# Context products of the first attention in two runs, and its running maxima read from the score banks

## The chip, the cores and the metric

The kernel runs on one core of a Trainium2 chip. The core has five engines that run beside each other and meet only at semaphores: TensorE (in the profile PE, with its weight loads apart as PEld), VectorE (DVE), ScalarE (ACT), GpSimd (POOL) and SyncE (SP), which here only starts transfers. [...] The metric is the time of one execution on the device, in microseconds.

## What is computed

The whole model has six layers. An input x of 16 samples with 64 rows of 512 passes through a cross-attention over a context (16 samples, 1601 keys of 256), a state-space layer, a routed feed-forward layer, a second cross-attention, a causal self-attention and a quantised gated feed-forward layer; each adds its result to x. The change touches only the first:

```python
def _L0_xattn_ref(q, k, v, Wq, bq, Wk, bk, Wv, bv, Wo, bo):
    HEADS, D_MODEL = 16, 512
    D_K = D_MODEL // HEADS
    B, LQ, _ = q.shape
    LKV = k.shape[1]
    qh = (q @ Wq + bq).reshape(B, LQ, HEADS, D_K).transpose(0, 2, 1, 3)
    kh = (k @ Wk + bk).reshape(B, LKV, HEADS, D_K).transpose(0, 2, 1, 3)
    vh = (v @ Wv + bv).reshape(B, LKV, HEADS, D_K).transpose(0, 2, 1, 3)
    scores = jnp.einsum('bhqd,bhkd->bhqk', qh, kh) * (1.0 / np.sqrt(D_K))
    attn = jax.nn.softmax(scores, axis=-1)
    out = jnp.einsum('bhqk,bhkd->bhqd', attn, vh)
    return out.transpose(0, 2, 1, 3).reshape(B, LQ, D_MODEL) @ Wo + bo
...
x = x + _L0_xattn_ref(_layernorm(x, axis=-1), ctx_512, ctx_512, ...)
```

## The kernel before, in words

All arithmetic is in fp32. The first attention is worked off in 32 units. Unit `u` is sample `u // 2` and one half of its heads, eight heads with 64 queries each, so a row of 512 scores per key. The 1601 keys are cut into 13 chunks `k` of 128 (the last has 65); keys lie on the partitions, and the tile `st` holds all scores of a unit as 13 chunks of 512 columns. There are two such tiles, so two units are in work at once.

The loop over `u` (its body begins at `for u in range(U + 1)`) is a pipeline over neighbouring units. In one turn the kernel builds the keys, values and scores of unit `u`, and finishes the softmax and the context of unit `u - 1`. The order of the instructions on each engine is written out by hand: `pin` keeps what it wraps in the order of the program. Every engine works strictly in that order, so an instruction that waits holds up all that is behind it on its engine.

One turn, in program order:

- `k_proj(u, i, z)` (L204 on TensorE, L218 on ScalarE): eight key products of 400 columns, each emptied by ScalarE into `kt`. Among them: `maxima(u-1)` transposes the running maxima on TensorE (L295) and VectorE reduces them over the keys (L297); `shift(u-1)` spreads the negated maxima on TensorE (L304) and VectorE adds them to the scores (L310); `exps(u-1, k)` takes the exponentials of two chunks on ScalarE (L318), and GpSimd adds them up in `acc` (L323, L325, L327). `divide(u-2)` (L351, L352) writes the normalised context of the unit before.
- `v_proj(u, k)` (L204, L229): 13 value products of 256 columns, each emptied by VectorE into `vt`. Key and value products share the two PSUM banks of the pool `ps_mm`, so a product starts only when the one before the last has been emptied.
- `scores(u, g)` (L204 on TensorE, tile `sc`): three groups of four chunks. A group fills four banks; then ScalarE copies it into `st` in two halves `r`, of four heads each (L264). The third group also does the short chunk 12 in `scl` (L268).
- `running_max(u, k)` on VectorE: the maximum over chunks, kept in `rm` as two chunks wide. `k == 2` starts it from chunks 0 to 3 (L284); 4, 6, 8 and 10 take two more chunks each from `st` (L286); 12 takes the short one (L289); L500 folds the two halves.
- `attend(u-1, i)` (tile `av<-st,vt`): context products, 13 chunks x 4 heads for each of the two halves `i`, each half 104 matmuls in the profile. Tiles of 32 columns of the array make them short. `sum_up(u-1)` adds the row sums from `acc` (`av<-acc,ones`), after L488 has folded `acc`.
- Beside that, one piece of the last layer's weights is quantised per turn: `piece_load` (SyncE), `piece_scale` (L164, L165, L166 on VectorE, L167 on GpSimd), `piece_round` (L171), `piece_store` (L175 on GpSimd, then SyncE).
- In seven of the turns `project(g)` takes two finished samples through the output projection (`ps<-wo,xnT`, L360) with the statistics of the next normalisation.

Every f32 matmul of keys, values, scores and context appears as two rows of the profile, so "x32" is a group of 16. [...]

## Time and profile before

| what | time |
|---|---|
| three timed runs, median (lowest to highest) | 2096.86 us (2092.23 to 2099.53) |
| the profiled execution itself | 2094.09 us |
| its span, first to last instruction | 2092.4 us |
| mean granted TensorE clock over the span | 0.985 |
| one ordinary unit, from first scores to first scores | 34.98 us |
| in that unit, busy: TensorE / VectorE / ScalarE / GpSimd | 33.41 / 27.60 / 17.05 / 19.73 us |
| mean of one maximum from `st` (L286, 128 of them) | 1678 ns |
| mean of one addition on GpSimd (L325, 124 of them) | 2575 ns |
| mean of one copy of scores (L264, 192 of them) | 1016 ns |

Rows of the profile give the line, the engine, the operation, output and inputs by tile name, the shape, the count, then busy time and the mean of one, and the idle time of the engine just before them with what ended it. A releaser "issue" means that the profile shows nothing that the engine waited for. In a timeline each row has start, duration, engine, line, operation, count, and in brackets the idle time before it. The loop over units runs from about 59 to 1215 us.

### The profile page before, as it was taken

What the parts mean: (1) busy time and instruction counts of PE and PEld (TensorE: products, weight loads), DVE (VectorE), ACT (ScalarE), POOL (GpSimd) and SP (SyncE); (2) the same over time, 40 slices, a digit from 0 to 9 for tenths busy, and PEclk for the clock granted to TensorE, in tenths of its full rate; (3) what the DMA queues carried; (4) which work ended last, traced back from release to release, by engine and by line L of the source; (5) the groups of instructions that cost most, each with busy time, mean ns of one, the idle gap of its engine ahead of it and who ended that gap; (6) DMA issues with size and microseconds to landing.
All of it is one profiled execution on the core that took longest, in us unless ns stands there. A gap on an engine that the chain in (4) does not pass through costs nothing. (4 is left out here: it accounts for less than half of the span.)

```text
span 2092.4 us, 39026 instructions
## 1 busy us (share of the span) xinstructions
PE 1958.8 (94%) x17197; PEld 1237.7 (59%) x17197; DVE 1262.7 (60%) x1741; ACT 801.3 (38%) x1112; POOL 713.1 (34%) x463
## 2 busy tenths in 40 slices
PE   8899999999999999999999799899999999999779
PEld 4677777677767677776767654444454455444334
DVE  2587778787787877787777844721113234428751
ACT  2445354545445453544445443210101133316700
POOL 0356555464546565564656421200003000000100
PEclk9999999999999999999999999999999999999879
DMA  5011001101110110111010120420227971200001
GB/s 204 21 54 43 32 32 53 43 17 48 43 53 11 53 43 22 43 50 46 12 53 11 37 102 22 168 76 19 94 67 280 347 295 61 71 0 11 20 0 40
DMA packets 61754, 141.13 MB, mean 67 GB/s; under 512 B 4448, under 2 KB 31600, under 8 KB 60432
## 3 DMA queue, kind: packets, MB, share of 16 engines
q1 hardware_dynamic: 61584, 138.63, 18.5%
q8 instruction: 135, 2.21, 0.4%
q14 instruction: 35, 0.29, 0.0%
HBM read 127.02 MB, written 11.60 MB: 66 GB/s over the span
## 5 line engine op out<-in xcount | busy, mean ns | idle before, releaser
L204 PE MATMUL ps<-wkv,ctxT 128*128 128x256 f32 (+1 forms) x1664 | 399.9, 388 | 26.9 <-DVE vt L229 25.6
L204 PE MATMUL ps<-ctxT,wkv 128*128 128x400 f32 (+1 forms) x1024 | 365.6, 504 | 9.7 <-DMA ctxT<-in_ctxT_dram 7.6
L204 PEld LDWEIGHTS ps<-wkv,ctxT 128*128 128x128 f32 (+1 forms) x1664 | 295.9, 185 | 107.4 <-DVE vt L229 38.0
L325 POOL TENSOR_TENSOR acc<-acc,st 128x1024 f32<-128x1024 f32 x124 | 319.3, 2575 | 23.6 <-ACT st L318 18.6
L218 ACT ACTIVATE kt<-ps,cols 128x400 f32<-128x400 f32 (+1 forms) x256 | 152.1, 594 | 372.5 <-PE ps L204 372.5
L229 DVE TENSOR_TENSOR vt<-ps,rows 128x256 f32<-128x256 f32 (+1 forms) x416 | 170.4, 420 | 183.9 <-PE ps L204 183.7
L264 ACT COPY st<-sc 128x1024 f32<-128x1024 f32 x192 | 185.0, 1016 | 246.8 <-PE sc L204 246.8
L204 PEld LDWEIGHTS ps<-ctxT,wkv 128*128 128x128 f32 x1024 | 190.0, 191 | 138.1 <-issue 9.3
L310 DVE TENSOR_TENSOR st<-st,nb 128x1024 f32<-128x1024 f32 (+1 forms) x224 | 239.1, 1139 | 34.6 <-PE nb L304 34.6
L318 ACT ACTIVATE st<-st 128x1024 f32<-128x1024 f32 (+1 forms) x224 | 215.9, 994 | 10.7 <-DVE st L310 10.4
L286 DVE TENSOR_TENSOR rm<-rm,st 128x1024 f32<-128x1024 f32 x128 | 214.8, 1678 | 2.2
L204 PEld LDWEIGHTS sc<-qd,kt 64*128 64x128 f32 x3072 | 178.9, 188 | 36.8 <-issue 24.5
L204 PE MATMUL sc<-qd,kt 64*128 64x128 f32 x3072 | 197.3, 278 | 2.1 <-ACT st L264 2.1
L323 POOL TENSOR_TENSOR acc<-st 128x1024 f32<-128x1024 f32 x31 | 73.4, 2367 | 311.0 <-issue 192.7
L204 PE MATMUL av<-st,vt 128*32 128x64 f32 x6656 | 106.8, 221 | 27.0 <-issue 18.0
L204 PEld LDWEIGHTS av<-st,vt 128*32 128x32 f32 x6656 | 98.5, 111 | 35.7 <-issue 26.7
L59 PE MATMUL ps<-xnT,w 128*128 128x512 f32 x256 | 112.2, 594 | 0.0
L59 PE MATMUL ps<-w,hT 128*128 128x512 f32 x256 | 110.2, 592 | 0.0
L167 POOL TENSOR_TENSOR w<-w,winv 128x512 f32<-128x512 f32 x36 | 48.4, 1346 | 163.6 <-DVE winv L166 152.8
L1200 POOL TENSOR_TENSOR gate<-up,gate 128x1024 f32<-128x1024 f32 x4 | 9.5, 2387 | 260.0 <-ACT up L1199 260.0
L276 POOL COPY qd<-xnT 32x128 f32<-32x128 f32 x128 | 79.4, 621 | 37.4 <-DVE xnT L395 32.4
L59 PE MATMUL po<-wdT,gate 128*128 128x512 f32 x192 | 85.4, 608 | 3.2 <-DVE gate L1222 3.2
(236 smaller groups left out, 2306.4 us busy)
## 6 DMA issues: line engine op xcount, KB each, us to landing
cT<-in_ctxT_dram SPq DMA_DIRECT2D x16, 1601.0 KB, 9.6
cN<-in_ctx_dram SPq DMA_DIRECT2D x16, 1536.0 KB, 9.8
ctxT<-in_ctxT_dram SPq DMA_DIRECT2D x15, 1601.0 KB, 7.3
grid<-w SPq DMA_DIRECT2D x36, 256.0 KB, 2.0
w<-grid SPq DMA_DIRECT2D x36, 256.0 KB, 2.7
w<-in_w_dram SPq DMA_DIRECT2D x2, 4096.0 KB
mk<-kept SPq DMA_DIRECT2D x16, 512.0 KB, 3.6
w<-in_wgate_dram SPq DMA_DIRECT2D x12, 256.0 KB, 3.2
```

The lines of the kernel that those rows point to most:

```text
L59: pe.matmul(out, lhsT=lhsT, rhs=rhs, start=start, stop=stop)
L167: pin(gp.tensor_tensor(w, w, inv.unsqueeze(2).to_broadcast([P, 16, 32]), ALU.mult))
L204: pin(pe.matmul(out, lhsT=lhsT, rhs=rhs, start=start, stop=stop))
L218: pin(s.activation(kts[u, i][:, o:o + n], ps[:, :n], AF.Identity, bias=col(C_BK0 + c)))
L229: pin(v.tensor_tensor(t[:n, :], ps[:n, :], row(R_BV0 + e, 256)[:n, :], ALU.add))
L264: pin(s.copy(st[:, ks[0]:ks[-1] + 1, r * 256:(r + 1) * 256], sc[:, r]))
L276: pin(gp.tensor_copy(qds[u % 2][r, :, (j % 2) * LQ:(j % 2 + 1) * LQ], qo[r, c:c + 2, b * LQ:(b + 1) * LQ]))
L286: pin(v.tensor_tensor(rms[u], rms[u], f[:, k:k + 2, :], ALU.max))
L310: pin(v.tensor_tensor(f[:m, k:k + n, :], f[:m, k:k + n, :], nb[:m].unsqueeze(1).to_broadcast([m, n, 512]), ALU.add))
L318: pin(s.activation(f[:m, k:k + n, :], f[:m, k:k + n, :], AF.Exp))
L323: pin(gp.tensor_tensor(accs[u], f[:, 0:2, :], f[:, 2:4, :], ALU.add))
L325: pin(gp.tensor_tensor(accs[u], accs[u], f[:, k:k + 2, :], ALU.add))
```

## The change

The score tile of a group becomes two tiles of two banks, one for each half `r`. The first group is treated as before. In the second and third group, VectorE no longer takes the maxima of chunks 4 to 11 from `st` but from the score banks, four instructions of 128x512 per group. Two engines don't read one tile at once: ScalarE copies half 1 while VectorE reads half 0, then they change over. The context products of half `i = 0` move from behind the third group to behind the second. The last exponentials of `u - 1` (chunk 12) move ahead of the second group's copies, and the fold of `acc` ahead of `piece_scale`.

```diff
-            sc = ps_sc.tile([P, 2, 4, 2 * P], F32, name="sc", tag="sc")
+            sc = [ps_sc.tile([P, 4, 2 * P], F32, name="sc", tag=f"sc{r}") for r in range(2)]
...
             for k in ks:
-                one_chunk([sc[:, r, k - ks[0], :] for r in range(2)], k)
+                one_chunk([sc[r][:, k - ks[0], :] for r in range(2)], k)
             if last == ks[-1] + 1:
                 tail = [ps_mx.tile([P, 2 * P], F32, name="scl", tag="mx"),
                         ps_mm.tile([P, 2 * P], F32, name="scl", tag="mm")]
                 one_chunk(tail, last)
-            for r in range(2):
-                pin(s.copy(st[:, ks[0]:ks[-1] + 1, r * 256:(r + 1) * 256], sc[:, r]))
+
+            def keep(r):
+                pin(s.copy(st[:, ks[0]:ks[-1] + 1, r * 256:(r + 1) * 256], sc[r]))
+
+            if g == 0:
+                keep(0)
+                keep(1)
+                return
+
+            keep(1)
             if last == ks[-1] + 1:
                 n = nkeys(last)
                 for r in range(2):
                     pin(s.copy(st[:n, last, r * 256:(r + 1) * 256], tail[r][:n]))
+            for r in range(2):
+                rm = rms[u][:, :, r * 256:(r + 1) * 256]
+                for z in (0, 2):
+                    pin(v.tensor_tensor(rm, rm, sc[r][:, z:z + 2, :], ALU.max))
+                if r == 0:
+                    keep(0)
...
                 pin(v.tensor_tensor(rms[u], f[:, 0:2, :], f[:, 2:4, :], ALU.max))
-            elif k + 1 < KC:
-                pin(v.tensor_tensor(rms[u], rms[u], f[:, k:k + 2, :], ALU.max))
             else:
...
             next_v(0, 1)
             scores(u, 0)
-            next_exps(2)
+            next_exps(3)
             next_v(2, 3, 4, 5)
             running_max(u, 2)
...
             scores(u, 1)
-            next_exps(1)
+            if old:
+                attend(u - 1, 0)
             next_v(6, 7, 8, 9)
-            running_max(u, 4)
-            running_max(u, 6)
-            if u < NPREP:
-                piece_scale(u, pin)
             if old:
                 acc = accs[u - 1]
                 pin(v.tensor_tensor(acc[:, 0], acc[:, 0], acc[:, 1], ALU.add))
+            if u < NPREP:
+                piece_scale(u, pin)
             if old and u <= NPREP:
                 piece_store(u - 1, pin)
             scores(u, 2)
             if old:
-                attend(u - 1, 0)
                 attend(u - 1, 1)
                 sum_up(u - 1, [(accs[u - 1][:, 0], P)])
-            running_max(u, 8)
-            running_max(u, 10)
             next_v(10, 11)
             running_max(u, 12)
```

## The prediction

> **What bounds the kernel now.** I read the shares of busy time first: TensorE is busy for 94% of the span (page line below), and the stretch from 100 to 1200 us, which is the first attention's loop, has 1051.6 us of matmul time in 1100.0 at a granted clock of 1.00. So the loop runs at the pace of TensorE, and a gain can only come from its idle time there. The list of waits in that stretch says whom it waits for (engine and line, released by whom: total us, times, longest):

> ```profile
> PE 1958.8 (94%) x17197; PEld 1237.7 (59%) x17197; DVE 1262.7 (60%) x1741; ACT 801.3 (38%) x1112; POOL 713.1 (34%) x463
> ...
> PE ps L204 <- DVE vt L229: 23.7, 24, 1.6
> ...
> PE av L204 <- issue: 18.9, 18, 1.7
> ```

> Two causes make almost all of it: value products that wait for VectorE to empty their bank, and a gap inside the context products. The timeline of one unit (start, duration) shows how they hang together:

> ```profile
> 557.85 2.06 PE L204 MATMUL sc<-qd,kt 64*128 64x128 f32 x32
> ...
> 563.03 5.67 POOL L325 TENSOR_TENSOR acc<-acc,st 128x1024 f32<-128x1024 f32 x2 [0.42 <-ACT st L318]
> ...
> 563.48 2.06 PE L204 MATMUL sc<-qd,kt 64*128 64x128 f32 x32
> ...
> 563.93 2.53 DVE L284 TENSOR_TENSOR rm<-st 128x1024 f32<-128x1024 f32 x1
> ...
> 565.47 3.72 PE L204 MATMUL ps<-wkv,ctxT 128*128 128x256 f32 x16
> ...
> 569.12 2.06 PE L204 MATMUL sc<-qd,kt 64*128 64x128 f32 x32
> ...
> 571.54 3.12 PE L204 MATMUL av<-st,vt 128*32 128x64 f32 x208
> ...
> 573.93 4.05 DVE L286 TENSOR_TENSOR rm<-rm,st 128x1024 f32<-128x1024 f32 x2
> ...
> 574.81 1.99 PE L204 MATMUL ps<-wkv,ctxT 128*128 128x256 f32 x8
> ...
> 577.91 0.74 DVE L229 TENSOR_TENSOR vt<-ps,rows 128x256 f32<-128x256 f32 x2
> 578.37 1.08 PE L204 MATMUL ps<-wkv,ctxT 128*65 128x256 f32 x4 [1.57 <-DVE vt L229]
> ```

> Call the start of the first scores (557.85) zero. The second scores start at 5.63, the third at 11.27, the context products at 13.69, value products 10 and 11 at 16.96. At 8 x 0.216 us of pitch, product 12 could start at 18.69. It starts at 20.52, because VectorE is in the last two maxima (4.05 us) and empties product 10 only at 577.91. The loss is **1.83 us per unit**. Another unit shows the gap:

> ```profile
> 645.24 0.59 PE L204 MATMUL av<-st,vt 128*32 128x64 f32 x26 [0.97 <-issue]
> ...
> 648.31 1.08 PE L204 MATMUL ps<-wkv,ctxT 128*65 128x256 f32 x4 [0.28 <-DVE vt L229]
> ```

> Its scores began at 627.81, so product 12 is at 20.50 again: the gap only eats up the wait. Taking the gap alone away would bring nothing; VectorE ends this stretch either way.

> **The change, part by part.** TensorE, GpSimd and SyncE keep their instructions (GpSimd's and SyncE's orders are untouched); of the 208 context products, 104 move behind the second scores. Per unit VectorE trades four 128x1024 maxima from SBUF for eight 128x512 ones that read PSUM.

> *Price of a maximum.* The old ones take 1687 ns on average, but the very first unit, with GpSimd idle, has the like at 1.23:

> ```profile
> 63.28 1.23 DVE L284 TENSOR_TENSOR rm<-st 128x1024 f32<-128x1024 f32 x1 [3.58 <-ACT st L264]
> ```

> The nearest row of the new form is L360, x<-x,ps 128x512, SBUF and PSUM operands: 686 to 689 ns in all 8, also where GpSimd adds beside it. A dependent VectorE instruction follows 0.035 behind, an independent one overlaps by 0.08 (rows L164, L165; L229). From the first of a group's four to the next eviction: 0.725 + 0.61 + 0.725 + 0.61 = **2.67 us**. Bounds: 2.3 (no better than four halves of the 1.13 pitch of L310) and 3.3 (half of 1687 each). I take 2.67. [...] New maxima have one SBUF input, and evictions of that kind keep 0.42 us in the middle of GpSimd's adds.

> *Second group.* Context half: 104 x 14.1 ns (2.93 us for 208) = 1.47. Scores at 5.63, context from 7.61, value products 6, 7 and 8 due at 9.13, 10.04 and 10.95. VectorE is still in L284 until 8.61, then runs the four maxima from 8.65, and empties product 6 at 11.32 to 11.74; product 8, in the same bank, starts at 11.78. Before, this eviction came at once. So **0.83 us of new stall** stands at product 8; third scores at 13.60 instead of 12.77.

> *Third group.* Tail scores 15.49, second context half 16.02, sums 17.49, product 10 at 17.82, product 12 due at 19.55. VectorE: evictions 8 and 9 until 14.2, the add of acc and the weight piece's scaling (0.63 + 1.15) until 15.85, maxima until 18.5, so it waits for product 10 and no stall is left. Product 12 starts at 19.55, 0.97 earlier. What is late next: the tail maximum and L500's fold (0.78 + 0.69) after eviction 11 end at 21.72; the transposes are due at 21.82 (k product after 0.92, 1.35 long). Before, they began at 22.79. I keep **0.9 us** per ordinary unit. From there the rest hangs on TensorE and just moves.

> *Units with an output projection* (7 of them): in the one begun at 662.77, second scores start at 9.07 and transposes at 26.84. By the same steps, the third scores come at 16.21, product 12 at 22.17, transposes at 24.44. The projection's VectorE work ends when the second scores do (about 11.2), so maxima end early enough that product 8 loses at most 0.1. Gain about **2.2 us** each.

> *New waits.* The third maximum waits for ScalarE's copy of its bank (ends 8.75 and 16.6; VectorE gets there at 9.98 and 17.2). ScalarE's held-back copy waits for the second maximum (10.0 and 17.2) and ends at 11.0 and 18.3. Behind it stand the next group's copy (15.6) and the k evictions (about 22); third scores need it at 13.6. All have over a microsecond, except that third maximum in group three, 0.6.

> *Moves at nothing.* The last exponential goes before the second copies: ScalarE is idle from 5.99 to 7.74 and it takes 0.64; the context half needs it at 7.61. Without that cover: 0.6 per unit. The add of acc moves ahead of the scaling; GpSimd's adds end at about 12.2, VectorE is there at 14.1. If GpSimd were late, scaling, maxima and evictions 10 and 11 would queue behind it. The scaled piece reaches GpSimd about 0.2 later, and its store and the next load on SyncE as much, with most of a unit to spare.

> *The gap.* A unit has 412 matmuls and as many loads, 824 instructions; the 135 packets of 16.4 KB on the instruction queue make about 255 TensorE instructions each. 824 is three packets and 56 more, and the gap indeed moves by about 30 products from unit to unit (after 202, 172, ...). It comes only when a packet's worth lies in the dense products (1.8 us). Halved, a packet spans at least 2.8 us; durations plus gaps ask for 2.2 to 3.2. I cost it at nothing. [...]

> **Sum.** 24 ordinary units x 0.9 = 21.6, 7 x 2.2 = 15.4, the first unit (no context products) about nothing: 37 us. The profiled execution took 2094.09 (span 2092.4), 2.8 under the median of 2096.86. 2094.1 - 37 = 2057; I say **2058**, between that and 2060 from the median.

> **Rivals.**
> - *Dearer maxima*: 3.3 us per group puts 0.6 more on product 8 in 24 units and some in the others, 18 in all: about 2076. For it: no row has exactly this form. Against: L360.
> - *The gaps stay*: another 18 or so lost, 2076. For it: half a run is still dense. Against: 2.8 us per packet.
> - *No stall at product 8*: if L284 gets ahead of GpSimd (1.23 instead of 2.53), 20 more are won: 2038. Against: GpSimd's pair starts at 5.18, L284 at 6.08, unit after unit.
> [...]
> - *The change isn't there*: the instruction orders show both halves and all eight maxima.

> **How the numbers follow.** Forecast 0.55 (own range 2049 to 2067), dearer maxima 0.12, gaps 0.08, no stall 0.07, lock or another wait that I don't see 0.18. The range 2038 to 2082 leaves that last one out. A measurement of this kernel tells about 0.3% (6 us) from no change; 0.04 of the favourable cases falls there: faster 0.78, same 0.04, slower 0.18.

> **What would show it.** Right: maxima of 0.69 us, product 8 waiting 0.7 to 0.9 for VectorE, no wait at product 12, no gaps among the context products, transposes about 0.9 earlier after a unit's first scores. Wrong: maxima over 0.85 us, gaps of a microsecond, or ScalarE's held-back copy delaying third scores.

## The result and the profile after

The change makes the kernel faster: the median of six runs is **2062.36 us** (2059.99 to 2070.21), against 2097.11 (2092.23 to 2099.53) in six runs of the kernel before. The ratio is 0.9842, with a 95% interval of 0.9823 to 0.9861. The medians are 34.7 us apart. The profiled execution took 2065.08 us (span 2063.4), which is 29.0 less than the profiled execution before; the sum of the prediction, 37, was made against that one. The profiled execution before was 3.0 faster than its median, the one after 2.7 slower, and the account below is of these two.

Of the 29.0, the loop holds 27.9. From the first unit's transposes of the maxima to the last unit's, 1115.7 us went by before, 1089.0 now, and the first transposes start 1.2 earlier. Over the same stretch (to the start of the last unit's first transpose) these are the length, then the busy time of TensorE, its weight loads, VectorE, ScalarE and GpSimd, and the granted clock, before and after:

```profile
80.55:1195.78 1115.23, 1068.87 (x12853) 793.76 (x12851) 868.89 (x1110) 539.49 (x727) 632.54 (x386) 1.00 0.10 36
...
79.34:1167.91 1088.57, 1068.47 (x12853) 792.15 (x12851) 824.00 (x1234) 542.69 (x727) 544.90 (x386) 1.00 0.11 37
```

TensorE is as busy as before, to 0.4 us; its idle time fell from 46.4 to 20.1, and these 26.3 are nearly all of the 26.7 by which the stretch is shorter. A unit's length, taken from its transposes to those of the next:

| interval between transposes (us) | before | after |
|---|---|---|
| ordinary units (22) | 34.98, four of them 35.93 to 36.04 | 34.22 to 34.30, the same four 34.98 to 35.29 |
| five of the seven with a projection | 38.08 or 38.09, one 39.04 | 36.77 to 36.83, one 37.72 |
| the other two with a projection | 39.04, 39.04 | 36.77, 36.77 |
| the unit behind each of these two | 35.93, 36.41 | 36.37, 36.83 |

The page of the kernel after, first busy times, then the row of the new maxima:

```profile
PE 1957.7 (95%) x17197; PEld 1236.0 (60%) x17197; DVE 1216.9 (59%) x1869; ACT 804.8 (39%) x1112; POOL 622.3 (30%) x463
...
L280 DVE TENSOR_TENSOR rm<-rm,sc 128x512 f32<-128x512 f32 x256 | 168.5, 679 | 10.7 <-PE sc L204 3.8
```

The line numbers have moved: L280 are the new maxima from the banks, L299 is the first group's maximum (L284 before), L331 the exponentials (L318), L338 GpSimd's additions (L325), L308 the transposes (L295), L509 the fold (L500); in the experiments some shift by a few lines. VectorE has 128 instructions more and 45.8 us less busy time: eight maxima of 679 ns replace four of about 1680. GpSimd's instructions are the same ones, and took 713.1 us before; what goes with that is seen in the part on the rivals. The list of waits in the kernel after, loop only (engine and line, released by whom: total us, times, longest):

```profile
PE ps L204 <- DVE vt L229: 14.9, 24, 0.6
...
PEld mt L308 <- DVE rm L509: 9.6, 30, 0.5
...
PEld av L204 <- issue: 5.3, 31, 0.2
```

Value products used to wait 23.7 us for VectorE; it is 14.9 now, one wait of 0.6 in each of 24 units. The gaps among the context products, 18.9 us before, are gone: only 0.2 at the first weight load of a run is left. The timeline of one ordinary unit of the kernel after (start, duration) shows where the wait has gone:

```profile
545.51 2.06 PE L204 MATMUL sc<-qd,kt 64*128 64x128 f32 x32
...
550.67 5.66 POOL L338 TENSOR_TENSOR acc<-acc,st 128x1024 f32<-128x1024 f32 x2 [0.40 <-ACT st L331]
...
551.14 2.06 PE L204 MATMUL sc<-qd,kt 64*128 64x128 f32 x32
...
551.59 2.52 DVE L299 TENSOR_TENSOR rm<-st 128x1024 f32<-128x1024 f32 x1
...
553.13 1.66 PE L204 MATMUL av<-st,vt 128*32 128x64 f32 x104
...
554.22 2.73 DVE L280 TENSOR_TENSOR rm<-rm,sc 128x512 f32<-128x512 f32 x4
...
556.86 0.75 DVE L229 TENSOR_TENSOR vt<-ps,rows 128x256 f32<-128x256 f32 x2
...
557.34 1.99 PE L204 MATMUL ps<-wkv,ctxT 128*128 128x256 f32 x8 [0.62 <-DVE vt L229]
...
559.26 2.06 PE L204 MATMUL sc<-qd,kt 64*128 64x128 f32 x32
...
563.49 2.86 PE L204 MATMUL ps<-wkv,ctxT 128*128 128x256 f32 x12
...
567.53 0.60 PE L308 MATMUL mt<-ident,rm 128*128 128x128 f32 x4
```

Read it from the wait in the middle. Product 8 (557.34) waits for an eviction, that is, for VectorE to empty product 6's bank (556.86). VectorE could not do that one sooner because it was in the four maxima of group two (554.22), and these began late because L299 had VectorE until 554.11. L299 runs beside GpSimd's pair of additions (550.67), as it did before. Product 10 to product 12, the place of the old stall, is now one unbroken run of 12 rows (563.49). So the stall was cut and moved from the third group to the second.

### The profile page after: what moved, and what is told of

It reads as the page before. It is cut to its first block, busy times and chain, and to the rows that moved or that the text cites. A ratio compares the mean times of both kernels' runs of the same rounds, so it can differ in the third digit from the quotient of the medians.

```text
span 2063.4 us, 39030 instructions
## 1 busy us (share of the span) xinstructions
PE 1957.7 (95%) x17197; PEld 1236.0 (60%) x17197; DVE 1216.9 (59%) x1869; ACT 804.8 (39%) x1112; POOL 622.3 (30%) x463
## 3 DMA queue, kind: packets, MB, share of 16 engines
q1 hardware_dynamic: 61584, 138.63, 18.9%
q8 instruction: 135, 2.21, 0.5%
## 5 line engine op out<-in xcount | busy, mean ns | idle before, releaser
L204 PE MATMUL ps<-wkv,ctxT 128*128 128x256 f32 (+1 forms) x1664 | 399.7, 388 | 16.5 <-DVE vt L229 16.3
L204 PE MATMUL ps<-ctxT,wkv 128*128 128x400 f32 (+1 forms) x1024 | 365.6, 503 | 12.7 <-DMA ctxT<-in_ctxT_dram 8.8
L204 PEld LDWEIGHTS ps<-wkv,ctxT 128*128 128x128 f32 (+1 forms) x1664 | 295.9, 185 | 96.2 <-DVE vt L229 26.8
L338 POOL TENSOR_TENSOR acc<-acc,st 128x1024 f32<-128x1024 f32 x124 | 319.6, 2577 | 23.0 <-ACT st L331 17.9
L265 ACT COPY st<-sc 128x1024 f32<-128x1024 f32 x192 | 191.7, 1016 | 320.5 <-PE sc L204 284.3
L229 DVE TENSOR_TENSOR vt<-ps,rows 128x256 f32<-128x256 f32 (+1 forms) x416 | 170.7, 421 | 202.0 <-PE ps L204 201.8
L204 PEld LDWEIGHTS ps<-ctxT,wkv 128*128 128x128 f32 x1024 | 189.7, 191 | 141.3 <-issue 12.8
L331 ACT ACTIVATE st<-st 128x1024 f32<-128x1024 f32 (+1 forms) x224 | 212.1, 992 | 7.3 <-DVE st L323 6.9
L204 PEld LDWEIGHTS sc<-qd,kt 64*128 64x128 f32 x3072 | 179.2, 188 | 36.5 <-issue 24.2
L204 PE MATMUL sc<-qd,kt 64*128 64x128 f32 x3072 | 197.8, 278 | 1.6 <-ACT st L265 1.6
L280 DVE TENSOR_TENSOR rm<-rm,sc 128x512 f32<-128x512 f32 x256 | 168.5, 679 | 10.7 <-PE sc L204 3.8
L204 PE MATMUL av<-st,vt 128*32 128x64 f32 x6656 | 108.7, 223 | 8.8 <-DVE xnT L365 8.8
L204 PEld LDWEIGHTS av<-st,vt 128*32 128x32 f32 x6656 | 98.5, 112 | 18.1 <-ACT st L331 9.1
L167 POOL TENSOR_TENSOR w<-w,winv 128x512 f32<-128x512 f32 x36 | 37.9, 1055 | 192.3 <-DVE winv L166 181.7
L59 PEld LDWEIGHTS ps<-w,hT 128*128 128x128 f32 x256 | 48.6, 190 | 61.2 <-issue 61.2
```

What stands on the lines that cost most here:

```text
L59: pe.matmul(out, lhsT=lhsT, rhs=rhs, start=start, stop=stop)
L167: pin(gp.tensor_tensor(w, w, inv.unsqueeze(2).to_broadcast([P, 16, 32]), ALU.mult))
L204: pin(pe.matmul(out, lhsT=lhsT, rhs=rhs, start=start, stop=stop))
L229: pin(v.tensor_tensor(t[:n, :], ps[:n, :], row(R_BV0 + e, 256)[:n, :], ALU.add))
L265: pin(s.copy(st[:, ks[0]:ks[-1] + 1, r * 256:(r + 1) * 256], sc[r]))
L280: pin(v.tensor_tensor(rm, rm, sc[r][:, z:z + 2, :], ALU.max))
```

## Experiments

Each kernel was timed beside runs of the kernel before. For the first four that ran (the context split alone, the maxima alone, both halves behind the second scores, values first) that took 2096.86 us, for the others 2094.97. Beside the medians I use the loop's length in the profile, first transposes to last: 1115.7 us before, 1089.0 after.

### One half of the change alone

*The context split without the new maxima.* The kernel before, with one half of the context behind the second scores and the exponentials moved ahead:

```diff
-            next_exps(2)
+            next_exps(3)
...
             scores(u, 1)
-            next_exps(1)
+            if old:
+                attend(u - 1, 0)
...
             if old:
-                attend(u - 1, 0)
                 attend(u - 1, 1)
```

> The kernel before, with only the context half i = 0 moved behind the second scores (and the last exponentials ahead of it); the maxima still come from st. Theory (VectorE's turn ends the stretch): the third scores start 1.5 us later, VectorE's chain behind them (two pairs of maxima of about 2.5 and 4.05 us, the scaling, the fold) begins later by as much, and product 12 starts at about 22.0 after the first scores of a unit instead of 20.52. 24 units x 1.5 and 7 x 0.5: about 2136 us, with no gaps left among the context products. Rival (the gain comes from breaking up the dense run): the gaps go and up to 19 us are won, 2078 to 2090.

It took 2168.17 us, ratio 1.0335 (1.0293 to 1.0378). The timeline of one of its units:

```profile
593.22 2.06 PE L204 MATMUL sc<-qd,kt 64*128 64x128 f32 x32
...
610.56 4.05 DVE L286 TENSOR_TENSOR rm<-rm,st 128x1024 f32<-128x1024 f32 x2
...
614.53 0.74 DVE L229 TENSOR_TENSOR vt<-ps,rows 128x256 f32<-128x256 f32 x2
615.00 1.08 PE L204 MATMUL ps<-wkv,ctxT 128*65 128x256 f32 x4 [1.95 <-DVE vt L229]
```

Product 12 starts 21.78 us after the unit's first scores, where the theory had 22.0 and the kernel before 20.52. The reason is seen in the rows: the pair of maxima (4.05 us) still stands ahead of the eviction, and TensorE has less context left with which to cover it. The unit is 36.24 long where nothing else disturbs it, 1.26 more than before; 31 such units are the 39 us of the theory. (This edit leaves the fold of `acc` behind the weight piece's scaling, so the sums also wait 0.53 for it in each unit; VectorE's eviction ends later still.) The measured loop is 77.2 longer, and the remaining 38 were on the list of neither theory. The granted clock in this loop is 0.97 and not 1.00, and 3.2% of its 1192 us is 38. The experiment on the clock comes back to it.

*The new maxima without the split.* The kernel after, with both halves of the context behind the third scores:

```diff
             scores(u, 1)
-            if old:
-                attend(u - 1, 0)
             next_v(6, 7, 8, 9)
...
             if old:
+                attend(u - 1, 0)
                 attend(u - 1, 1)
```

> The kernel after, with the context half i = 0 moved back behind the third scores. Theory: without 1.5 us of context products between the second scores and product 6, product 8 is due at 9.4 and still waits for VectorE until 11.8, a stall of 2.4 us; the whole run of context products is dense again, VectorE no longer hides its gaps, so about 1 us comes on top in some 18 units. Product 12 at about 21.1 in units without a gap against 20.52 before: 24 x 0.55 + 18 - 3 makes about 2125 us. Rival (cheaper maxima alone pay): VectorE's relief of 1.8 us per unit shows as time, 2060 to 2080.

It took 2157.65 us, ratio 1.0291 (1.0265 to 1.0317). In the timeline of a unit, the wait at product 8:

```profile
596.15 2.88 PE L204 MATMUL ps<-wkv,ctxT 128*128 128x256 f32 x8 [2.22 <-DVE vt L229]
```

The four maxima are the same as in the kernel after, but no context product lies between scores and value products, so TensorE stands for 2.2 us instead of 0.6. The dense run of 208 context products is back too, and with it 18.9 us of gaps in the list of waits. Each half alone is about 3% slower than the kernel before, and a good part of that is a lowered clock (below: 1.95% is left of the maxima's 2.9% when it is kept up); together they are 1.6% faster. The maxima free VectorE at the end of the unit and load it in the middle; the context half fills the middle.

### Where the context products stand, and the gaps

*Both halves behind the second scores*, which makes the run of 208 whole again but leaves everything else as it is after the change:

```diff
             if old:
                 attend(u - 1, 0)
+                attend(u - 1, 1)
             next_v(6, 7, 8, 9)
...
             if old:
-                attend(u - 1, 1)
                 sum_up(u - 1, [(accs[u - 1][:, 0], P)])
```

> The kernel after, with both context halves behind the second scores, so 208 in one run. Theory on the gaps (an instruction packet that lies in the dense run takes longer to come than to be used): gaps of about a microsecond return among the context products in some 18 of 31 units, VectorE's chain behind is moved by each, and about 15 to 19 us are lost against the kernel after: 2078 to 2082. Product 8 no longer waits, but product 12 does, by about as much, so units without a gap keep their length. Rival (the gaps came from something at the end of the unit, not from density): no gaps, 2055 to 2063.

It took 2091.76 us, ratio 0.9975 (0.9965 to 0.9985); almost all of the gain is gone. Its list of waits in the loop:

```profile
PE av L204 <- issue: 18.9, 21, 1.4
```

and the timeline of a unit with such a gap:

```profile
563.51 2.66 PE L204 MATMUL av<-st,vt 128*32 128x64 f32 x174
...
567.32 0.72 PE L204 MATMUL av<-st,vt 128*32 128x64 f32 x34 [1.15 <-issue]
```

The gap is inside the run, no data is waited for, and it stands in 21 units of 31. Ordinary units without one are 33.98 long in most cases, 0.24 shorter than in the kernel after; those with a gap of 0.3 to 0.6 us are 34.6 to 34.8, those with one of 0.8 to 1.2 are 35.2 to 35.6. The same products in two runs have none, and no version with two runs showed one. So in these kernels the length of the dense run decides on the gap.

What goes with a gap is seen in the transfers of the trace. The page has a DMA queue of kind "instruction" with 135 packets, 2.21 MB, so 16.4 KB each. In each of the 18 gaps of the kernel before and the 21 of this one, exactly one such packet lands 1.2 to 1.6 us before the gap ends; the same holds for the 20 and 18 gaps of the two kernels of the next section. A moment taken at random stands at that distance from a packet in 4% of cases. From the start of the packet to the end of the gap 2.2 to 2.9 us go by. That agrees with gaps that are waits for instructions, as the prediction worked out from its counts; no run changed the packets themselves, so it is not shown as the cause.

The loss is 29 and not the 15 to 19 that I had expected: a unit with a gap is longer by more than the gap lasts. I put that down to the place of the gap, ahead of evictions, so that VectorE's work is pushed back with it; that is not shown.

### What lowers the clock

In the loop of maxima_only TensorE is busy for 1097.6 us with the work for which the kernel before takes 1068.9, and the granted clock is 0.98. About a microsecond after the end of the wait above the clock falls to half, for 3.41 us; that is why the eight rows took 2.88 us and not 1.99. Of 24 waits of 2.2 us in the loop, 16 are followed by such a drop; of seven with 1.2 to 1.3, none. These 16 drops cost about 27 us (16 x 3.41 at half speed).

Why 16 of 24? The drops lie on a fixed grid: in all ten traces every change of the granted clock stands within 0.004 us of a multiple of 3.413 us, counted from the first. Here is the step of the grid that holds the wait above and the step behind it, then two such steps around another wait (columns: stretch, its length, busy time of TensorE, its weight loads, VectorE, ScalarE and GpSimd with counts, granted clock, DMA share, GB/s):

```profile
593.69:597.10 3.41, 1.19 (x6) 0.87 (x5) 2.67 (x6) 1.01 (x1) 2.72 (x2) 1.00 0.00 0
597.10:600.51 3.41, 3.41 (x19) 2.54 (x19) 1.86 (x4) 0.00 (x0) 0.00 (x0) 0.50 0.02 5
214.84:218.25 3.41, 1.44 (x7) 0.94 (x5) 3.24 (x6) 1.61 (x2) 3.33 (x2) 1.00 0.00 0
218.25:221.66 3.41, 3.17 (x30) 2.68 (x32) 2.08 (x6) 0.00 (x0) 0.58 (x1) 1.00 0.00 0
```

Both waits last 2.2 us, but the second one lies across the edge of two steps: its part in this one is 1.94 us. Counted by steps, the loops of all ten traces agree. Each of the 38 drops (16 here, 22 in split_only, behind waits of 1.95 us) follows a step in which TensorE stood idle for 1.95 us or more, and no step with 1.94 or less has a drop behind it.

To see whether it is the standing still that does it, I took maxima_only and put four more matmuls between value products 7 and 8. They write to the context bank, which the context products then overwrite, and so add work and no result:

```diff
-            next_v(6, 7, 8, 9)
+            next_v(6, 7)
+            if old:
+                avs[u - 1] = ps_av.tile([P, 2, 2, LQ], F32, name="av", tag="av")
+                for _ in range(4):
+                    pmm(avs[u - 1].rearrange("p a i q -> p (a i q)"),
+                        ctxT[u // 2][:, 0, 0:P], wkv0[:, 1, 0, 0:256])
+            next_v(8, 9)
```

> The kernel of maxima_only (maxima from the banks, context products whole behind the third scores) with four more matmuls of 256 columns per unit between value products 7 and 8, into the bank of the context, where they are overwritten; they compute nothing that is used. They last about 1.7 us and lie inside the 2.2 us wait at product 8. Theory (that wait is long enough for TensorE's clock to be lowered behind it, which cost maxima_only about 30 us more than its stalls): with the wait filled the granted clock stays at 1.00 in the loop, and the time falls to about 2125 us although there is more to do. Rival (the extra came from something else): 2155 to 2170.

It took 2136.32 us, ratio 1.0195 (1.0168 to 1.0222): 21 less than without the additional work, both intervals well apart. In the same columns, a long stretch of this kernel:

```profile
100.00:600.00 500.00, 484.14 (x5780) 363.88 (x5779) 353.97 (x538) 226.99 (x305) 235.39 (x170) 1.00 0.12 39
```

and of maxima_only:

```profile
100.00:600.00 500.00, 462.11 (x5410) 342.10 (x5408) 350.12 (x526) 225.07 (x301) 234.04 (x164) 0.98 0.11 38
```

The wait is down to 0.48 us, the clock at 1.00 throughout the loop, and all groups of eight rows take 1.99 us again; the loop is 26.2 shorter, near the 27 of the drops. So for maxima_only the lowered clock is shown as the cause of these 20 us. For split_only no run filled the wait; its drops too stand behind steps with 1.95 us of idle time, and 22 of them at half speed are 38 us, what its theory missed. Both kernels miss the 2125 of the theory, maxima_fill by 11, for which gaps that push VectorE's chain back, as in the experiment above, are a guess.

### What is left at product 8

By the prediction, the 0.8 us at product 8 come from the order on VectorE and from the length of the first group's maximum. That one (L299) took 1.23 us in the first unit (64.93), with GpSimd idle, and 2.52 in the unit above beside GpSimd's pair of additions; that pair took 5.66, the pair of the same unit without such a maximum beside it (545.48) 4.79. Two experiments on the kernel after take one of these each.

*Order.* Products 6 and 7 with their evictions ahead of the context half and of the maxima of group two (`between` is called in `scores` behind `keep(1)`):

```diff
-            scores(u, 1)
+            scores(u, 1, lambda: next_v(6, 7))
             if old:
                 attend(u - 1, 0)
-            next_v(6, 7, 8, 9)
+            next_v(8, 9)
```

> The kernel after, with value products 6 and 7 (and their evictions on VectorE) ahead of the context half and of the second group's maxima. Theory: the 0.8 us stall at product 8 is only a matter of order and goes away, nothing else moves; third scores at about 12.8 after a unit's first scores instead of 13.6, transposes about 0.75 earlier, 24 units x 0.7: about 2045 us. Rival (VectorE is full there anyway): the maxima then end at 12.7 and the third scores wait for them or product 10 does, and the time stays within 5 us of 2062.

It took 2050.47 us, ratio 0.9774 (0.9748 to 0.98); the loop is 1073.8 long, 15.2 less than in the kernel after. The timeline of a unit that begins at 537.52:

```profile
547.07 1.66 PE L204 MATMUL av<-st,vt 128*32 128x64 f32 x104
547.17 0.42 DVE L229 TENSOR_TENSOR vt<-ps,rows 128x256 f32<-128x256 f32 x1 [0.44 <-PE ps L204]
547.52 2.72 DVE L282 TENSOR_TENSOR rm<-rm,sc 128x512 f32<-128x512 f32 x4
...
548.66 1.99 PE L204 MATMUL ps<-wkv,ctxT 128*128 128x256 f32 x8
...
550.58 2.06 PE L204 MATMUL sc<-qd,kt 64*128 64x128 f32 x32
```

Both banks are emptied as the maxima begin, so product 8 (548.66) finds its bank free; the third scores come 13.06 after the first instead of 13.75. An ordinary unit is 33.53 to 33.59.

*The first maximum.* The first group's maximum, called locked in the expectation for its 2.5 us beside GpSimd, in two halves, each with one operand from the score bank, between the evictions of products 2, 3 and 4, instead of L299 behind product 5:

```diff
+        def first_max(u, r):
+            if r == 0:
+                rms[u] = mxp.tile([P, 2, 512], F32, name="rm", tag="rm")
+            c = slice(r * 256, (r + 1) * 256)
+            pin(v.tensor_tensor(rms[u][:, :, c], sts[u][:, 0:2, c], scs[u][r][:, 2:4, :], ALU.max))
...
-            next_v(2, 3, 4, 5)
-            running_max(u, 2)
+            next_v(2)
+            first_max(u, 0)
+            next_v(3)
+            first_max(u, 1)
+            next_v(4, 5)
```

> The kernel after, with the first group's maximum no longer taken from st in one 128x1024 instruction (2.5 us beside GpSimd), but as two of 128x512 with one operand in the score banks, placed between the evictions of value products 2, 3 and 4. Theory (the 0.8 us stall at product 8 is the tail of that locked instruction): VectorE is free when the second scores are ready, the maxima end at about 10.4 after a unit's first scores, product 8 doesn't wait, about 2048 us, and GpSimd's pair beside it takes 4.8 instead of 5.7 us. Rival (VectorE is late for another reason, or the earlier work stalls products 4 and 5 instead): 2058 or more.

It took 2050.57 us, ratio 0.9794 (0.9758 to 0.9831); the loop is 1068.0, 21.0 less than in the kernel after, and no value product waits for VectorE in the loop. So either way the whole wait at product 8 is gone: by order (14.9 of the 15.2 are TensorE's idle time), or here, where 14.9 of the 21.0 are idle time and the other 6 are shorter busy time of TensorE in the same instructions (1062.4 against 1068.5). What makes that shorter has not been tried. Nor does this edit isolate what GpSimd beside it costs, since it changes the form and the place of the maximum at once.

*The fold.* In the kernel after, the weight load of the transposes waits for L509, the fold of `rm` (9.6 us in all in the list of waits). If that wait costs anything, the fold should move ahead of evictions 10 and 11, with the short chunk's maximum behind it:

```diff
+            pin(v.tensor_tensor(rms[u][:, 0], rms[u][:, 0], rms[u][:, 1], ALU.max))
             next_v(10, 11)
             running_max(u, 12)
-            pin(v.tensor_tensor(rms[u][:, 0], rms[u][:, 0], rms[u][:, 1], ALU.max))
```

I tried it on both versions. On the one with values first:

> The kernel of values_first, with the fold of the two halves of the running maxima moved ahead of value evictions 10 and 11. Theory (each unit's transposes wait 0.2 to 0.3 us for tail maximum and fold): the fold then runs while VectorE waits for product 10, and 31 x 0.2 = 6 us are won: about 2044 us. Rival (the fold delays eviction 10 and so product 12 by as much): 2050 or a little more.

It took 2049.72 us, ratio 0.978 (0.9754 to 0.9806), the same as without it, with a loop of 1072.6 against 1073.8. So this expectation fell: the waits for the fold are gone from the list and ordinary units stay at 33.53, because the weight load waited beside key products that were still running. On the version with the first maximum from the banks:

> first_banks together with the early fold of values_fold. Theory: both add up, about 2042 us. Rival: the fold gains nothing here, as first_banks.

It took **2045.30 us** (2043.78 to 2047.06), ratio 0.9762 (0.9737 to 0.9786), and is the fastest of all. Its loop is 1066.8, 1.2 less than without the fold, of which 0.7 in the last unit; the 5 us between the two medians are more than that, and their intervals overlap, so that a gain from the fold (about 2042 was expected for the two together) is not shown. Timeline of a unit that begins at 537.95:

```profile
541.44 0.68 DVE L299 TENSOR_TENSOR rm<-st,sc 128x512 f32<-128x512 f32 x1
...
542.37 0.68 DVE L299 TENSOR_TENSOR rm<-st,sc 128x512 f32<-128x512 f32 x1
...
543.11 4.84 POOL L346 TENSOR_TENSOR acc<-acc,st 128x1024 f32<-128x1024 f32 x2 [0.38 <-ACT st L339]
...
545.67 2.73 DVE L282 TENSOR_TENSOR rm<-rm,sc 128x512 f32<-128x512 f32 x4 [1.55 <-PE sc L204]
...
547.16 3.72 PE L204 MATMUL ps<-wkv,ctxT 128*128 128x256 f32 x16
```

The 2.52 us of L299 have become 2 x 0.68, done before GpSimd's pair begins, and that pair takes 4.84 instead of 5.66. VectorE now waits for the scores (1.55), and not TensorE for VectorE: products 6 to 9 are one run of 16 rows. In a long stretch of the loop TensorE has no idle time left:

```profile
100.00:600.00 500.00, 500.00 (x6140) 374.25 (x6139) 370.67 (x597) 248.81 (x336) 249.67 (x183) 1.00 0.13 44
```

An ordinary unit is 33.33 us, about the busy time of TensorE in a unit of the kernel before (33.41). From waits there is hardly anything left to win in this loop.

## Why the prediction was right, and where its sizes were off

The forecast was 2058 us, the median came out at 2062.36, within its own range. By the profiled pair, 29.0 us were won where the sum had 37, so the mechanism was right and its two largest terms too big; that the median still came so near is in part the luck of the two medians, which are 5.7 further apart than the profiled pair. Step by step:

- *TensorE's idle time in the loop is what can be won, and VectorE ends the last stretch of a unit.* Right. The whole gain of the loop is TensorE's idle time. With hardly any left (4.4 us in the loop of first_fold), the loop follows the busy time of TensorE.
- *Price of the new maxima.* Right. 679 ns on average against the 0.69 taken from L360; the four of group two hold VectorE for 2.73 us, those of group three for 2.67 (forecast 2.67 for both), also where GpSimd adds beside them.
- *0.83 us of new stall at product 8.* Right, in place and size: product 6 at 9.21 after the first scores (forecast 9.13), product 8 at 11.83 (11.78). The idle time of TensorE that the profile shows in front of it is 0.62, a little under the 0.7 to 0.9 that the prediction named as its sign.
- *No stall at product 12, and ScalarE's held copies with slack.* Right: in the loop no engine waits for either.
- *0.9 us per ordinary unit.* A term too large: 22 ordinary units gained 16.43 us, 0.75 each. In the unit shown, the third scores stand at 13.75 (forecast 13.60) and the transposes at 22.02 (21.82). By product 8, 0.05 had been lost, and 0.10 more between product 8 and the third scores. I had let these begin on the ideal pitch behind a stall and behind a change from context tiles to full ones. What makes them late by a tenth has not been tried.
- *2.2 us per projection unit.* The term that failed most. The unit that I had worked through, begun at 662.77, gained 2.26 as forecast (39.04 to 36.77). But I took it as the type of all seven, and five of them gain only 1.26 to 1.33. The two that gain 2.26 and 2.28 hold the table load of ScalarE's square root (L119), and the unit behind each of them loses 0.44 and 0.41. Here is the unit worked through, in the kernel before, and beside it (391.89) the same pair of maxima in a common projection unit:

```profile
675.88 1.28 ACT L318 ACT_TABLE_LOAD   x1
677.18 0.63 ACT L318 ACTIVATE st<-st 65x512 f32<-65x512 f32 x1
677.92 3.43 DVE L286 TENSOR_TENSOR rm<-rm,st 128x1024 f32<-128x1024 f32 x2
677.95 2.32 POOL L327 TENSOR_TENSOR acc<-acc,st 65x512 f32<-65x512 f32 x1 [4.35 <-ACT st L318]
...
391.89 2.48 DVE L286 TENSOR_TENSOR rm<-rm,st 128x1024 f32<-128x1024 f32 x2
```

The last exponential stood behind the square root and so needed its own table back. It came 1.4 late (14.41 after the unit's first scores instead of 12.98), GpSimd's addition of it fell onto VectorE's pair, and the pair took 3.43 instead of 2.48. That is about the 0.96 by which this unit was longer than a common one, and it went away with the change for a reason that the sum had put at nothing: the last exponential now runs ahead of the square root. The table is then loaded back in the unit behind:

```profile
652.13 2.53 ACT L331 ACTIVATE st<-st 128x1024 f32<-128x1024 f32 x3
654.67 1.28 ACT L119 ACT_TABLE_LOAD   x1
...
680.83 1.28 ACT L331 ACT_TABLE_LOAD   x1
...
683.72 1.61 PE L204 MATMUL ps<-ctxT,wkv 128*128 128x400 f32 x4 [0.91 <-ACT kt L218]
```

It stands right before the next unit's first exponential, the evictions of keys queue up behind it, and a key product waits for one. In split_only, which also moves the last exponential, the second load falls into the unit behind too (742.55, with the first at 711.81). All seven together gained 11.08 us against the 15.4 of the sum, and the units behind gave 0.85 back.

- *Nothing in the first unit.* It won 1.2, against nothing in the forecast; another 1.1 came outside the loop. Neither has been traced.
- *The balance.* Ordinary units: 15.6 (16.43 less the 0.85 given back) against 21.6, so 6.0 less; projection units 4.3 less; first unit and the rest 2.3 more. That is 8.0 less than 37: 29.0.
- *The gaps vanish.* Right for the run in halves that the text spoke of; whole again, the run costs more than the 18.9 us that its gaps last.

The rivals: *dearer maxima* and *the gaps stay* did not happen. *No stall at product 8* did not happen by itself; first_banks, with that maximum out of GpSimd's way, agrees with it: the loop is 21 us shorter, where the rival had put 20. The *lock* among the chances, new maxima drawn out beside GpSimd as the first group's is, did not show: the four at 554.22 ran beside GpSimd's pair of additions (until 556.33) and took 2.73 us, as in the first unit (66.83) with GpSimd idle. GpSimd's side shows a difference as well. Its rows by shape, in the loop of the kernel before:

```profile
L276 POOL COPY qd<-xnT 32x128 f32<-32x128 f32 x120 | 75.8, 632 | 4.7
...
L175 POOL TENSOR_TENSOR w<-w,wsc 128x512 f32<-128x512 f32 x30 | 60.7, 2024 | 0.0
```

and of the kernel after:

```profile
L290 POOL COPY qd<-xnT 32x128 f32<-32x128 f32 x120 | 34.3, 286 | 4.7
L175 POOL TENSOR_TENSOR w<-w,wsc 128x512 f32<-128x512 f32 x31 | 32.5, 1050 | 0.0
```

The products of L175 lie beside VectorE's maxima in both kernels, the copies in part. Both take half as long since these read one operand from the score banks, and that goes with the maxima and not with the place of the context: in split_only they take 627 and 2025 ns, in maxima_only 287 and 1051. Whether that operand or the smaller instruction does it, no run takes apart.

## What to carry to other kernels

Taking load from the engine that ends a stretch, and moving work into a stretch that thereby stalls, can each lose and together win: work out both places before either is tried alone. When one unit stands for many in a sum, look through the lengths of all units first, and take the price from the commonest kind. When you move an activation past one that needs another table, follow where the table is loaded back. When TensorE stands still, look at the granted clock before you put a loss down to the wait alone; in these loops, steps with at most 1.94 us of idle time never lowered it.

## What of the hardware was not expected

The cost of a dense run was the other surprise. In runs of 208 short matmuls (both_second) TensorE stood still in 21 gaps of 0.9 us on average, 18.9 us in the list of waits, each ending 1.2 to 1.6 us behind the landing of an instruction packet, and a loss of 29 us. Two runs of 104 with other products between them have none.
